# Interleaved scans of a two-layer MetaFormer: other slots for column copies, gate products and output products

## The chip, the cores and the metric

The kernel runs on one core of one Trainium2 chip. The metric is the device time of one execution in microseconds. The kernel before took 1302.23 us, the median of 3 runs (1301.95 to 1303.36).

The core has five engines that run side by side and meet at semaphores: TensorE (PE in the profile), VectorE (DVE), ScalarE (ACT), GpSimd (POOL) and SyncE (SP), which here issues the DMAs. Each works through its own list of instructions in the order in which the program emits them.

## What is computed

Two layers of a MetaFormer on an image of 64 by 64 positions with 96 channels. Each layer is a state-space mixer ("conv") and a small quantized MLP ("ffn"), each with a norm ahead of it and a residual sum behind it. The change touches the mixer of layer 1 and the end of the stage ahead of it. Cut to what matters:

```python
xz = x @ W_in.T
xp, z = xz[..., :192], xz[..., 192:]
xc = silu(conv3x3(xp) + conv_b)                      # all 192 channels to all
x_hw = xc.reshape(B, 192, L)                         # by rows, L = 4096
x_wh = transpose(xc, (0, 1, 3, 2)).reshape(B, 192, L)   # by columns
xs = [x_hw, x_wh, flip(x_hw), flip(x_wh)]            # four directions
x_dbl = einsum('bdl,cd->bcl', xs, x_proj_w)          # step rank 6, B 16, C 16
delta = softplus(dt_proj_w @ x_dbl[:, :6] + dt_proj_b)
# for each channel d and each of 16 states n, along L:
#   h = exp(delta * A) * h + (delta * u) * B
#   y = sum_n h * C
y = scan(...) + D * xs
yy = (y0 + back(y1) + flip(y2) + back(flip(y3))) * silu(z)
out = x + yy @ W_out.T
```

192 channels times 16 states times 4 directions are 12288 recurrences of 4096 steps.

## The kernel before

**Passes.** A pass handles 32 channels and 4 states, on 128 partitions; 6 groups of channels times 4 passes are 24 passes (i = 0 to 23, group g = i // 4, k = i % 4). In a pass two chains run: the row chain (o = 0) and the column chain (o = 1), each forward and then backward over the 4096 steps. A step of a chain (e = 0 to 7) is one DVE scan over 1024 positions, so a pass has 16 scans and the kernel 384.

**The sequence of scans.** The list `seq` (L1891 to L1896) interleaves the two chains: the column chain leads and the row chain follows two steps behind. Position p in `seq` is a scan. `base[i]` is 16i - 2, and the text calls position `base[i] + s` slot s of pass i; slots 16 and more of a pass are slots 0 and more of the next.

**What goes with a scan.** For every p the program emits `scan(p)` for DVE, then `decay(p + 1)` for ACT (the exponential that the next scan needs, L1947), then what the dictionary `plan` holds for p (L2187). A step with e = 4 needs no decay of its own; these are the scans in slots 8 and 13. There are two buffers for decays (`two`), so a decay waits until the scan before the last has ended. As engines take their instructions in order, an instruction put at slot s stands on its own engine in front of everything that is put later.

**The operations that `put` places:**
- `permute(i, a)` (L1936, ACT): copies a quarter of B*du from row order into column order, into `xw`, for the column chain of pass i. It needs all of `xs` of that pass and must wait until `add_columns` of the pass before has read that quarter of `xw`.
- `times_b` (L1930, POOL): B times du, for the next pass but one quarter at a time.
- `add_columns` (L1964, POOL): adds both directions of the column chain, back in row order, into `hs`. It is put at the scan of step NS + a of the column chain.
- `add_rows`, `add_hs`, `add_all` (L1970, L1974, PE): sum both directions of the row chain and `hs` by products with the identity, into two PSUM buffers; `fetch` (L1983, ACT) copies them out; `times_c` (L1987, POOL) multiplies by C; `sum_states` (L1998, PE) adds the states into the accumulator of the group.
- Once in a group: `skip`, `fetch_y`, `store` (L2051, L2057, L2065).
- The gate of a group, in four parts (b, e), two in pass k = 1 and two in pass k = 2: `load_z` (L2025, SP), `product_z` (L2030, PE), `tanh_z` (L2039 to L2041, three operations on ACT), `silu_z` (L2045, POOL). `load_z` writes into the buffer that also holds the group's y until it is stored.
- The early output products of passes 17 to 23: `load_y` (L2075, SP), `early_out` (L2082, L2084, PE), `early_fetch` (L2088, ACT).
- Loads: `load_c` (L1926), `load_part` (B, L1853), `load_du`, `load_dt` (L1909), all issued by SP.

**The stage ahead of the scans.** Layer 0's end, layer 1's convolution and projections are emitted by a planner, `Order`. Every operation has an engine, a cost, what it reads and writes, and for a DMA its size. `run` emits, one at a time, the operation that can start first, and of those that can start at the same time the one of highest rank: the cost of the longest chain of operations that follows, plus a hand-written lead (`LEAD`). The scans stand in this plan as a chain of dummy operations on an engine "SCAN" (`first_pass`, L1213), each with the keys that it needs; so they give rank to what they need.

`project` (L1633) computes, for a unit of 1024 positions, B, C, the step sizes (softplus) and step times u. Channels 0 to 127 are "wide", 128 to 191 "narrow". `by_column` (L1732) also turns the step sizes into column order: the wide ones into `dtc[0]`, the narrow ones into `dtc[1]`. These two lie in the buffers `hs` and `h0` of the scans (L1178). After the last unit:
- `columns(j)` spreads quarter j of the first 32 channels' column steps into `dt1` (L1826);
- `load_b(1, ...)` loads B for pass 1 into `xs(1)` (L1827);
- `store_columns` (L1829) stores the rest of `dtc[0]` and all of `dtc[1]` for later groups.
The row chain's first scan writes `h0`, and so waits until `dtc[1]` has been stored.

Of the kernel before, what the change touches and what calls it, by code (L numbers as in the profile page):

```python
# [39 lines left out]
P = 128  # L40
HW = 64
L = HW * HW
NJ = L // P
CD = 96
DI = 192
# [204 lines left out]
class Net:  # L250
# [962 lines left out]
    def first_pass(self):  # L1213

        o = self.order  # L1220
        pairs = [(c, m) for c in (0, 4) for m in range(2)]
        needs = {0: [("xs0", c) for c in range(NCH)] + [("dt1", k) for k in range(2)] + ["rates"]}
        needs |= {1: [("dt1", 2), ("dt1", 3)]} | {j: [("dt1s", j)] for j in range(2, NS)}
        needs |= {2 * NS: [("DT", p) for p in pairs]}
        needs |= {3 * NS: ["xs1"] + [("DU", p) for p in pairs]}
        needs |= {6 * NS: ["sdtc"] + [(k, p) for k in ("sdt", "sdu", "sdtn", "sdun") for p in pairs]}
        for s in range(6 * NS + 1):
            o.add("SCAN", 2.35, lambda: None, r=needs.get(s, []), w=["scans"])
# [404 lines left out]
    def project(self, c, m, last):  # L1633
# [147 lines left out]
        o.add("SP", 0.65, store_du, r=[du, ("du", n, 0), ("du", n, 1)], w=[("sdu", n)], kb=512)  # L1781
        if m == 1:
            both = [(c, 0), n]
            o.add("SP", 0.65, first_group(lambda: self.dt0, self.dt_d[0]), r=[("sdt", p) for p in both], w=[("DT", p) for p in both], kb=1024)
            o.add("SP", 0.65, first_group(lambda: self.du, self.du_d), r=[("sdu", p) for p in both], w=[("DU", p) for p in both], kb=1024)
# [41 lines left out]
        o.add("SP", 0.65, lambda: self.load_b(1, xs(1), slice(0, L)), r=["xs", *(("B", p) for p in ((0, 0), (0, 1), (4, 0), n))], w=["xs1"], kb=2048)  # L1827

        def store_columns():  # L1829
            keep(dma(self.dt_d[1][GC:P], self.dtc[0][GC:P]))  # L1830
            keep(dma(self.dt_d[1][P:DI], self.dtc[1]))

        narrow = [("dtcn", p, k) for p in ((0, 0), (0, 1), (4, 0), n) for k in range(2)]
        o.add("SP", 1.3, store_columns, r=every + narrow, w=["sdtc"], kb=2560)
# [20 lines left out]
    def scans(self, xs, out):  # L1855
# [14 lines left out]
        with ExitStack() as ctx:  # L1870
# [20 lines left out]
            lead, both, end = 5, 2 * NS, [(1, 4), (1, 5), (0, 2), (1, 6), (1, 7), (0, 3)]  # L1891
            chain = [[(i, o, e) for i in range(n) for e in range(both)] for o in range(2)]
            stop = both * last + 4
            seq = [s for m in range(both * n) for s in (chain[1][m : m + 1] if m < stop else [])
                   + (chain[0][m - 2 : m - 1] if 2 <= m < stop else [])]
            seq += [(last, o, e) for o, e in end] + chain[0][both * last + NS :]  # L1896
# [193 lines left out]
            for f, i0, spots in (  # L2090
                (0, n - 7, ((0, 10, 12), (2, 12, 13))),
                (1, n - 3, ((1, 9, 10), (2, 11, 12), (4, 12, 13))),
            ):
                for m in range(NCH):
                    i, s = divmod(m, len(spots))
                    for do, at_slot in zip((load_y, early_out, early_fetch), spots[s]):
                        early.setdefault((i0 + i, at_slot), []).append((do, (f, m)))
# [13 lines left out]
            for g in range(NG):  # L2111
                for b in range(2):
                    for e in range(2):
                        for f, s in zip((load_z, product_z, tanh_z, silu_z), ((0, 9, 10, 11), (10, 13, 14, 15))[e]):
                            early.setdefault((NK * g + 1 + b, s), []).append((f, (g, b, e)))
# [14 lines left out]
            for i in range(n):  # L2130
# [11 lines left out]
                else:  # L2142
# [8 lines left out]
                    spots(i, sum_states, 19, 22, 23, 26)  # L2151
                    if k == NK - 1:
                        for f, s in ((skip, 26), (fetch_y, 29), (store, 31)):
# [3 lines left out]
                if i:  # L2157
                    for j, s in enumerate((-1, 2, 4, 7)):
                        put(at + s, times_b, i, j)
                    for a, s in enumerate((12, 13, 15, 20)):  # L2160
# [19 lines left out]
            permute(0, 1)  # L2180
# [287 lines left out]
```

## Time and profile before

| | |
|---|---|
| profiled execution | 1301.16 us, span 1299.2 us |
| median of the runs | 1302.23 us |
| stage ahead of the scans | 0 to 329.7 us |
| scans (DVE L1959) | 329.76 to 1222 us |
| tail (output product, MLP of layer 1) | 1222 to 1299.2 us |
| DVE busy | 1142.2 us (88%) |
| PE busy | 1053.5 us (81%) |
| ACT busy | 895.1 us (69%) |
| POOL busy | 844.1 us (65%) |
| mean granted TensorE clock | 0.849 |

A scan takes 2.26 to 2.35 us, and in a full row of them one starts every 2.24 us. Times of the timeline are microseconds from the start of the span. A line of it has start, duration, engine, line of the kernel, operation, what it writes and reads with their shapes, how often, and in brackets the idle time of the engine before it with what ended it. Tile names end in s where the program has several of a kind: `h0s` is `h0`, `hss` is `hs`, `xws` is `xw`; `da` is a decay, `kept` stands for buffers of layer 0 that the scans use again.

### The profile page before, as it was taken

How to read it: one execution, taken by the hardware profiler on the slowest of the kernel's cores; microseconds unless marked ns; L12 is line 12 of the kernel's file. 1: busy time of each engine (PE TensorE's matmuls, PEld its weight loads, DVE VectorE, ACT ScalarE, POOL GpSimd, SP SyncE). 2: the span in 40 equal slices, each digit the busy share in tenths (PEclk: the TensorE clock that was granted, in tenths of full speed). 3: DMA queues.
4: the chain of work that ended last, by engine and by line, in shares of the span. 5: the costliest groups of instructions: out<-in, count | busy, mean ns of one | idle time of the engine just before them, and what ended most of it. 6: DMA issues, size and time to landing. Idle time of an engine off the chain costs nothing. (4 is left out here: it accounts for less than half of the span.)

```text
span 1299.2 us, 11492 instructions
## 1 busy us (share of the span) xinstructions
PE 1053.5 (81%) x3654; PEld 435.4 (34%) x3654; DVE 1142.2 (88%) x899; ACT 895.1 (69%) x1085; POOL 844.1 (65%) x516
## 2 busy tenths in 40 slices
PE   9998988996088777777878877778779887999875
PEld 7632333331033222222223322222224333434443
DVE  6395798668799999999999999999998999999775
ACT  4445656554578877877787877777777877677345
POOL 3000574523578888787888879778887778774445
PEclk9999989985588787888898878878889888888855
DMA  2053010347844483566545473557454474524001
GB/s 72 18 162 98 2 25 13 110 158 237 287 123 131 148 264 123 173 206 204 201 147 175 144 245 100 168 203 232 172 170 157 142 262 129 175 75 130 8 7 43
DMA packets 78912, 183.18 MB, mean 141 GB/s; under 512 B 21503, under 2 KB 34905, under 8 KB 77657
## 3 DMA queue, kind: packets, MB, share of 16 engines
q1 hardware_dynamic: 78152, 182.16, 44.2%
q8 instruction: 31, 0.51, 0.2%
q14 instruction: 41, 0.33, 0.1%
q10 hardware_dynamic: 688, 0.19, 0.1%
HBM read 159.73 MB, written 21.52 MB: 140 GB/s over the span
## 5 line engine op out<-in xcount | busy, mean ns | idle before, releaser
L1987 POOL TENSOR_TENSOR kept<-kept,kept 128x1024 f32<-128x1024 f32 x92 | 216.9, 2357 | 95.0 <-issue 49.4
L1964 POOL TENSOR_TENSOR hss<-h1s,xws 128x1024 f32<-128x1024 f32 x96 | 228.0, 2375 | 77.0 <-DVE xws L1959 74.7
L1970 PE MATMUL hs<-h0s,ident 128*128 128x512 f32 x376 | 229.3, 695 | 48.4 <-DVE h0s L1959 34.7
L1947 ACT ACTIVATE da<-dt1s,a 128x1024 f32<-128x1024 f32 x168 | 187.6, 1117 | 71.3 <-DVE xws L1959 58.6
L1959 DVE TENSOR_TENSOR_SCAN xws<-da,xws 128x1024 f32<-128x1024 f32 x96 | 222.3, 2315 | 9.7 <-ACT da L1947 9.5
L1947 ACT ACTIVATE da<-dt0s,a 128x1024 f32<-128x1024 f32 x168 | 187.9, 1119 | 54.8 <-DVE h0s L1959 31.3
L1974 PE MATMUL hs<-hss,ident 128*128 128x512 f32 x376 | 190.3, 598 | 3.0 <-POOL hss L1964 2.9
L1998 PE MATMUL acc<-kept,fold 128*32 128x512 f32 x384 | 102.3, 715 | 100.4 <-POOL kept L1987 97.0
L1959 DVE TENSOR_TENSOR_SCAN h1s<-da,h1s,xws 128x1024 f32<-128x1024 f32 x72 | 167.7, 2330 | 3.2 <-ACT da L1947 3.0
L1983 ACT COPY kept<-hs 128x512 f32<-128x512 f32 x188 | 109.6, 583 | 64.3 <-PE hs L1974 63.7
L1970 PEld LDWEIGHTS hs<-h0s,ident 128*128 128x128 f32 x376 | 73.5, 215 | 177.8 <-issue 106.1
L1974 PEld LDWEIGHTS hs<-hss,ident 128*128 128x128 f32 x376 | 71.6, 192 | 100.4 <-issue 83.8
L1930 POOL TENSOR_TENSOR x1s<-x1s,dus 128x1024 f32<-128x1024 f32 x32 | 75.6, 2364 | 12.0 <-DMA dus<-du 12.0
L1970 PE MATMUL hs<-x1s,ident 128*128 128x512 f32 x128 | 74.2, 664 | 8.3 <-DVE x1s L1959 8.3
L1970 PE MATMUL hs<-x0s,ident 128*128 128x512 f32 x128 | 72.5, 651 | 9.6 <-DVE x0s L1959 9.6
L1959 DVE TENSOR_TENSOR_SCAN x2s<-da,x2s 128x1024 f32<-128x1024 f32 x32 | 74.2, 2320 | 5.3 <-ACT da L1947 4.9
L1959 DVE TENSOR_TENSOR_SCAN x0s<-da,x0s 128x1024 f32<-128x1024 f32 x32 | 74.2, 2317 | 4.7 <-ACT da L1947 4.7
L1959 DVE TENSOR_TENSOR_SCAN x1s<-da,x1s 128x1024 f32<-128x1024 f32 x32 | 74.2, 2318 | 4.5 <-ACT da L1947 4.5
L1930 POOL TENSOR_TENSOR x2s<-x2s,dus 128x1024 f32<-128x1024 f32 x32 | 75.9, 2371 | 0.0
L1970 PE MATMUL hs<-x2s,ident 128*128 128x512 f32 x120 | 66.9, 642 | 5.0 <-DVE x2s L1959 5.0
L1238 POOL MEMSET pairs<- 96x256 f32 x1 | 0.3, 307 | 103.1 <-ACTq L303 103.1
L1930 POOL TENSOR_TENSOR x0s<-x0s,dus 128x1024 f32<-128x1024 f32 x28 | 66.2, 2365 | 0.0
(346 smaller groups left out, 1976.8 us busy)
## 6 DMA issues: line engine op xcount, KB each, us to landing
kept<-bc SPq DMA_DIRECT2D x92, 512.0 KB
x2s<-bc SPq DMA_DIRECT2D x32, 512.0 KB
x0s<-bc SPq DMA_DIRECT2D x28, 512.0 KB
x1s<-bc SPq DMA_DIRECT2D x28, 512.0 KB
dus<-du SPq DMA_DIRECT2D x20, 512.0 KB
dt1s<-dt SPq DMA_DIRECT2D x20, 512.0 KB
dt0s<-dt SPq DMA_DIRECT2D x20, 512.0 KB
kept<-xn SPq DMA_DIRECT2D x24, 384.0 KB
```

Source lines behind the costliest of these rows:

```text
L1238: nc.gpsimd.memset(self.pairs1[:, :, 0 : HW + 2 : HW + 1, :], 0.0)
L1930: keep(nc.gpsimd.tensor_tensor(x, x, du[:, part[j]], ALU.mult))
L1947: keep(nc.scalar.activation(t, dts[o][:, part[j]], AF.Exp, scale=self.a6[:, g, k : k + 1]))
L1959: keep(nc.vector.tensor_tensor_scan(to, da, x, start, ALU.mult, ALU.add))
L1964: keep(nc.gpsimd.tensor_tensor(cols(hs)[:, w, :], grid(h1)[:, w, :], grid(xw)[:, w, :], ALU.add))
L1970: keep(nc.tensor.matmul(t, self.ident, x[:, chunk(m)], start=x is h0, stop=False))
L1974: keep(nc.tensor.matmul(sums[i, m], self.ident, hs[:, chunk(m)], start=False, stop=True))
L1983: keep(nc.scalar.copy(to, sums.pop((i, j * (SC // CH) + h))))
L1987: keep(nc.gpsimd.tensor_tensor(t, t, times_c_by(i, a), ALU.mult))
L1998: keep(nc.tensor.matmul(to, self.fold4, src, start=k == 0, stop=k == NK - 1))
```

## The change

- *First pass.* Its sequence is written out (`first`): the row chain starts after four column scans instead of three, and two of its scans follow each other. From pass 1 on the sequence and `base` are as before.
- *First column copies.* The second one of pass 0 is made by DVE instead of ACT.
- *Narrow step columns.* `store_columns` becomes two operations: the narrow part, in two halves, which needs the narrow copies alone, and the wide part. The load of B for pass 1 becomes two halves. The second half, and the last unit's load of du, also name the narrow copies among what they read.
- *Dummy scans of the planner.* 23 of 2.25 us instead of 25 of 2.35 us, with other needs at other positions.
- *Slots.* `permute` 12 to 11; `sum_states` 26 to 27; `skip` 26 to 24; `fetch_y` 29 to 28; the gate's two parts from (0, 9, 10, 11) and (10, 13, 14, 15) to (3, 7, 8, 9) and (8, 12, 12, 13); the early output products of passes 17 to 20 from (0, 10, 12), (2, 12, 13) to (5, 9, 10), (7, 10, 11), and of passes 21 to 23 as in the diff.

```diff
@@ first_pass
         needs = {0: [("xs0", c) for c in range(NCH)] + [("dt1", k) for k in range(2)] + ["rates"]}
-        needs |= {1: [("dt1", 2), ("dt1", 3)]} | {j: [("dt1s", j)] for j in range(2, NS)}
-        needs |= {2 * NS: [("DT", p) for p in pairs]}
-        needs |= {3 * NS: ["xs1"] + [("DU", p) for p in pairs]}
-        needs |= {6 * NS: ["sdtc"] + [(k, p) for k in ("sdt", "sdu", "sdtn", "sdun") for p in pairs]}
-        for s in range(6 * NS + 1):
-            o.add("SCAN", 2.35, lambda: None, r=needs.get(s, []), w=["scans"])
+        needs |= {1: [("dt1", 2), ("dt1", 3)], 2: [("dt1s", 2)], 3: [("dt1s", 3)]}
+        needs |= {4: ["sdtcn"] + [("DT", p) for p in pairs[0:2]]}
+        needs |= {8: [("DT", p) for p in pairs[2:4]]}
+        needs |= {5: [("xs1", 0)] + [("DU", p) for p in pairs[0:2]], 7: [("xs1", 1), "sdtc"] + [("DU", p) for p in pairs[2:4]]}
+        needs |= {22: [(k, p) for k in ("sdt", "sdu", "sdtn", "sdun") for p in pairs]}
+        for s in range(23):
+            o.add("SCAN", 2.25, lambda: None, r=needs.get(s, []), w=["scans"])
@@ project
+        narrow = [("dtcn", p, k) for p in ((0, 0), (0, 1), (4, 0), n) for k in range(2)]
         if m == 1:
             both = [(c, 0), n]
...
-            o.add("SP", 0.65, first_group(lambda: self.du, self.du_d), r=[("sdu", p) for p in both], w=[("DU", p) for p in both], kb=1024)
+            o.add("SP", 0.65, first_group(lambda: self.du, self.du_d), r=[*(("sdu", p) for p in both), *(narrow if last else [])], w=[("DU", p) for p in both], kb=1024)
...
-        o.add("SP", 0.65, lambda: self.load_b(1, xs(1), slice(0, L)), r=["xs", *(("B", p) for p in ((0, 0), (0, 1), (4, 0), n))], w=["xs1"], kb=2048)
-
-        def store_columns():
-            keep(dma(self.dt_d[1][GC:P], self.dtc[0][GC:P]))
-            keep(dma(self.dt_d[1][P:DI], self.dtc[1]))
-
-        narrow = [("dtcn", p, k) for p in ((0, 0), (0, 1), (4, 0), n) for k in range(2)]
-        o.add("SP", 1.3, store_columns, r=every + narrow, w=["sdtc"], kb=2560)
+        for h in range(2):
+            half = slice(h * L // 2, (h + 1) * L // 2)
+            o.add("SP", 0.65, lambda half=half: self.load_b(1, xs(1), half), r=["xs", *(("B", p) for p in ((0, 0), (0, 1), (4, 0), n)), *(narrow if h else [])], w=[("xs1", h)], kb=1024)
+
+        def store_columns(g, parts):
+            rows = (slice(GC, P), slice(P, DI))[g]
+
+            def f():
+                for i in range(parts):
+                    s = slice(i * L // parts, (i + 1) * L // parts)
+                    keep(dma(self.dt_d[1][rows, s], self.dtc[g][GC * (1 - g) :, s]))
+
+            return f
+
+        o.add("SP", 1.3, store_columns(1, 2), r=narrow, w=["sdtcn"], kb=1024)
+        o.add("SP", 0.65, store_columns(0, 1), r=every + narrow, w=["sdtc"], kb=1536)
@@ scans
-            lead, both, end = 5, 2 * NS, [(1, 4), (1, 5), (0, 2), (1, 6), (1, 7), (0, 3)]
+            both = 2 * NS
             chain = [[(i, o, e) for i in range(n) for e in range(both)] for o in range(2)]
-            stop = both * last + 4
-            seq = [s for m in range(both * n) for s in (chain[1][m : m + 1] if m < stop else [])
-                   + (chain[0][m - 2 : m - 1] if 2 <= m < stop else [])]
-            seq += [(last, o, e) for o, e in end] + chain[0][both * last + NS :]
+            first = [(1, 0), (1, 1), (1, 2), (1, 3), (0, 0), (1, 4), (0, 1), (1, 5), (0, 2), (0, 3), (1, 6), (0, 4), (1, 7), (0, 5)]
+            end = [(1, 4), (1, 5), (0, 2), (1, 6), (1, 7), (0, 3), *((0, e) for e in range(NS, both))]
+            seq = [(0, o, e) for o, e in first]
+            for m in range(both, both * last + NS):
+                seq += [chain[1][m], chain[0][m - 2]]
+            seq += [(last, o, e) for o, e in end]
...
-                (0, n - 7, ((0, 10, 12), (2, 12, 13))),
-                (1, n - 3, ((1, 9, 10), (2, 11, 12), (4, 12, 13))),
+                (0, n - 7, ((5, 9, 10), (7, 10, 11))),
+                (1, n - 3, ((2, 9, 10), (5, 10, 11), (7, 13, 14))),
...
-                        for f, s in zip((load_z, product_z, tanh_z, silu_z), ((0, 9, 10, 11), (10, 13, 14, 15))[e]):
+                        for f, s in zip((load_z, product_z, tanh_z, silu_z), ((3, 7, 8, 9), (8, 12, 12, 13))[e]):
...
-                    spots(i, sum_states, 19, 22, 23, 26)
+                    spots(i, sum_states, 19, 22, 23, 27)
                     if k == NK - 1:
-                        for f, s in ((skip, 26), (fetch_y, 29), (store, 31)):
+                        for f, s in ((skip, 24), (fetch_y, 28), (store, 31)):
...
-                    for a, s in enumerate((12, 13, 15, 20)):
+                    for a, s in enumerate((11, 13, 15, 20)):
                         put(at + s, permute, i, a)
...
-            permute(0, 1)
+            permute(0, 1, nc.vector.tensor_copy)
```

## The prediction

> **What bounds the kernel now.** I read the page's busy table first, then who waited for whom, then the groups of VectorE (DVE), and last the timelines around the largest waits. The chain that ended last covers only the tail of the program and says nothing about the scans.
>
> ```profile
> DVE  6395798668799999999999999999998999999775
>   ACT da L1947: 28.0, 34
>   DMA dt<-h0s: 5.1, 1
> ```
>
> From slice 10 on DVE is nearly full: it runs 384 scans, started one every 2.24 us (two chains take turns), from 329.76 to 1222 us. The other two lines are the view of the scan line: before a scan DVE sat idle 28.0 us for a decay from ScalarE (ACT) and 5.1 us for one DMA. So the scans' missing starts are the whole prize here. I took the start times of all 384 scans from the trace and summed what each step exceeds 2.24 us by. The sum is 34.8 us. I place it by pass i and slot s (scan number 16i-2+s):
> - the first three steps: 6.5
> - slot 1 of passes 2, 3, 6, 7, 10, 11, 14, 15 (after a pass that computed a gate): 2.8, and slot 2 of pass 15: 1.0
> - slot 15 of passes 4, 8, 12, 16: 2.8
> - passes 17 to 23, where early output products are mixed in: 20.8
> - the last scans, which depend on each other: 1.0
>
> The start:
>
> ```profile
> 329.76 2.29 DVE L1959 TENSOR_TENSOR_SCAN h1s<-da,xws 128x1024 f32<-128x1024 f32 x1 [1.41 <-ACT da L1947]
> 332.68 2.35 DVE L1959 TENSOR_TENSOR_SCAN h1s<-da,h1s,xws 128x1024 f32<-128x1024 f32 x1 [0.63 <-ACT da L1947]
> 335.58 2.35 DVE L1959 TENSOR_TENSOR_SCAN h1s<-da,h1s,xws 128x1024 f32<-128x1024 f32 x1 [0.55 <-ACT da L1947]
> 343.01 2.29 DVE L1959 TENSOR_TENSOR_SCAN h0s<-da,x0s 128x1024 f32<-128x1024 f32 x1 [5.08 <-DMA dt<-h0s]
> 345.21 2.33 DVE L1959 TENSOR_TENSOR_SCAN h1s<-da,h1s,xws 128x1024 f32<-128x1024 f32 x1
> ```
>
> The row chain's first scan writes h0s, which still holds the narrow step columns, and waits until their store has landed. How a slot gets late on ACT:
>
> ```profile
> 436.56 0.37 ACT L2039 COPY kept<-z 128x256 f32<-128x256 f32 x1
> 436.82 0.38 ACT L2040 ACTIVATE kept<-z 128x256 f32<-128x256 f32 x1
> 437.23 0.51 ACT L2041 ACTIVATE kept<-kept,columns 128x256 f32<-128x256 f32 x1
> 437.65 1.10 ACT L1947 ACTIVATE da<-dt1s,a 128x1024 f32<-128x1024 f32 x1
> 438.69 1.98 ACT L1936 COPY xws<-x0s 128x1024 f32<-128x1024 f32 x1
> 440.57 1.11 ACT L1947 ACTIVATE da<-dt0s,a 128x1024 f32<-128x1024 f32 x1
> ```
>
> Start to start, a gate's three operations take 1.2, a decay 1.05, a column copy 1.9. A decay may start when the scan two before its own has ended, so a slot holds one decay and 1.2 of other work; slots 7 and 12 have no decay to make and are free. The gate in slot 14 between copies in 13 and 15 is too much, and the decay at 440.57 ends after its scan was due. Worst, pass 17:
>
> ```profile
> 978.75 0.48 ACT L2088 COPY res<-eo 128x384 f32<-128x384 f32 x1 [5.66 <-PE eo L2084]
> ```
>
> ACT stands at a copy whose TensorE (PE) product is late, and the decay behind it starts at 979.13; the scan waits 4.00 us.
>
> **What the Trainium skill says.** *PSUM — Partial Sum Buffer* (Engine vs sequencer instructions): the queues of ScalarE, VectorE and GpSimdE are strict FIFO, and matmuls run in program order. The trace agrees (the decay behind the 5.66 us wait). *DMA: Bandwidth & Descriptors* (Anatomy of one DMA): about 2.0 us plus bytes at 436 GB/s. From the issue at 328.61, the three queued loads and stores are 3.5 MB, an estimate of 10.4 us by that page; the scan was released at 343.0, after 14.4, so I use the trace's rate. *TensorE: Matmul & The Clock Gate* (What's actually happening): an idle array falls to half clock after about 3.4 us. The trace agrees: 0.43 us a matmul in a run, 1.04 after a 3.96 us wait.
>
> **The change, part by part.**
>
> 1. *Narrow columns stored first, row chain one later, second column copy on DVE.* The copy (1.03) fits in the 1.41 us that DVE idles before scan 0. ACT then makes the second decay at once: scans 0 to 2 start at 329.76, 332.0, 334.3. ACT next does decay 1.05, copy 1.9, decay, copy, decay: the fourth decay ends near 336.9, so scan 3 starts there and scan 4 (the first of the row chain) at 339.2, against 345.21 for scan 4 before: 6.0 gained. It needs the narrow store landed by 339.2. POOL ends the narrow copies at 330.40. The trace's packets show dt0s (1 MB) moving from 331 to 335 and 16 KB stores at 0.38 MB/us, so 1 MB right behind it ends at 337.7, plus about 1 to land: just in time. Against it: the loads of du's second half and of xs1's second half queue behind these stores. GpSimd (POOL) multiplies them (2.34 each) and in its queue the first column sum (2.36) stands between; the copy for pass 1 on ACT, now due about 6 us sooner, needs all three. Before, du landed at 348.36. If both land then, the copy can start at 355.4; ACT can wait until 354.0 without making a decay late: 1.4 lost. At 347 nothing, at 352 about 5. I take 1.0 with a doubled scan (0.15): **gain 5.0**, ends 1 and 6.
>
> 2. *Second gate half from slots 13/14 to 12/12, its load from 10 to 8.* In slot 12 ACT has no decay to make: column copy to 12+0.9, gate to about 13+0.4, decay, copy to 14+1.1, next decay by 14+2.2, on time. The load goes ahead of one du part and one xs part in SP's queue, which removes the 3.96 us for which PE waited on kept<-xn in pass 2. The slot 1 and slot 2 excess goes: **gain 3.7**.
>
> 3. *First gate half from 9/10 to 7/8, its load from 0 to 3.* Here I see a new wait:
>
> ```profile
> 422.09 1.02 PE L1974 MATMUL hs<-hss,ident 128*128 128x512 f32 x2
> 423.05 1.06 PE L1998 MATMUL acc<-kept,fold 128*32 128x512 f32 x8
> 423.93 0.62 PE L2030 MATMUL z<-kept,wz 96*32 96x256 f32 x8
> ```
>
> PE comes to this product without a gap; it is 18.3 us of matmuls behind the first fetch. Nothing stands between slots 7 and 9 in PE's order, so it ends where it ended: 424.55, slot 9+1.0 (9+0.75 when slot 1 is no longer late). But ACT is now to read it in slot 8, ahead of the decay for slot 10. Then gate 1.2, decay 1.05: 1.0+1.2+1.05-2.24 = 1.0 us late. Queued behind it: that decay, the fetch of slot 9, and DVE for both. Twelve passes do it (k = 1 and 2 of six groups); eight of them lie outside the late passes: **loss 8**. Ends: 0 if PE is 1.0 earlier than I think, 16 if it is 1.0 later. The earlier load lets load_c go before the wait for the stored y; POOL's 4 to 5 us waits for kept<-bc in passes 5, 9, 13, 17 go, off the path. The gates' POOL products (0.72) move to 9 and 13, ahead of a column sum; POOL is 82% busy (493 of 602 us) and no scan waits for it.
>
> 4. *Group end: skip 26 to 24, fetch of y 29 to 28, last sum_states 26 to 27.* The fetch (0.9) moves into free slot 12, so slot 15 of passes 4, 8, 12, 16 is on time: **gain 2.8**. The first column copy from 12 to 11 is issued in the same ACT gap, only ahead of that fetch.
>
> 5. *Early products at slots 9, 10 (and 13), ahead of the last sum_states.* PE no longer stands at the sum (POOL) before them. They follow the gate product or the last fetch: 2.7 us each warm. Their loads move from 0 and 2 to 5 and 7, still 9 us ahead of use; the slowest load near there, xn in pass 2 (issued 424.78, its product 434.39), took 9.6, so at worst the first is 0.6 late. In 19 and 20 ACT finds both in time: 0 left of 5.0. In 17, 18, 21, 22 the new wait of part 3 comes first (1.0), the first product is then 0.3 late for its copy, and the second pushes the gate of slot 12 to about 12+2, leaving 0.8 in slots 14/15: 2.1 each, 8.4 together of 20.8: **gain 12.4**, ends 6 and 18.
>
> 6. *Order of the stage before.* The planner ranks operations by what follows; almost everything leads to scan 0 and shifts alike. What rises are the narrow softplus, its POOL copies and DT and DU loads (the store was due at scan 24, now 4). No trace row prices that. PE's conv chain, which ends near 291, sets this stage; I take 0, ends -4 (the last narrow operations stand behind 2.3 and 1.7 us waits now) and +4.
>
> Sum: 5.0+3.7-8.0+2.8+12.4 = 15.9. The profiled execution took 1301.16 (1.96 more than its span), so 1285.3; it lies 1.07 under the median of the runs, so I forecast **1286**.
>
> **Rivals.**
> - *No new wait in slot 8.* PE runs the gate product sooner and ACT finds it ready. For it: fetches could come earlier. Against: PE has no gap to close from slot 1 to 9. The 8 and 4 us return: 1274.
> - *The start is given back.* du and xs1 land at 352 and ACT waits for POOL at the first copy of pass 1: 5 less gain. For it: 1.5 MB of wide columns are stored ahead of them. Against: xs1's first load is half as long. 1291.
> - *Slower.* The new ranks put narrow softplus of the earlier units ahead of conv work on ACT and DVE; conv's PSUM banks are freed later, PE's chain of 72 products stalls, and scan 0 starts late by the same amount. From 15.9 us late it decides; DVE's longest waits there now are 7.4 and 12.4 us, so two such are enough. 19 us late gives 1305. Against it: up to 329.7 us ACT is busy 54% and DVE 71% (177.4 and 234.0 of 329.7 us).
>
> **How the numbers follow.** The forecast (own range 1280 to 1290) gets 0.50, no wait in slot 8 0.19, start given back 0.16, slower 0.10; 0.05 for sums that cancel. A measurement here tells about 0.2% (2.6 us) from no change. Faster 0.85, same 0.05, slower 0.10. The range 1273 to 1297 takes in the first rivals and the ends of parts 1, 3 and 5, and leaves out about 2 in 10.
>
> **What would show it.** In the new trace: scan 4 near 339 with no wait for dt<-h0s (part 1); no scan late in slots 1 and 15 of passes up to 16 (2, 4); scans late by 1 us in slot 10 of passes 1, 2, 5, 6, with ACT's L2039 copy waiting for PE z (3); no 4 us wait in pass 17 (5); scan 0 at 330 +-4 (6). A first scan past 345, or gate waits of 2.5 us, would make the prediction wrong.

## The result and the profile after

The changed kernel took 1298.63 us (median of 20 runs, 1287.6 to 1302.33), the kernel before 1302.45 us (20 runs on the same chips, 1296.88 to 1304.54). The ratio is 0.9967 with a 95% interval of 0.9951 to 0.9983: 0.33% faster. The forecast was 1286, its range 1273 to 1297. The profiled execution of the changed kernel took 1298.4 us, its span 1296.6.

The page's busy strip of DVE and, from the view of the scan line, what DVE sat idle for before a scan (us in all, times):

```profile
DVE  7394788558799999999999999999999999999775
...
  ACT da L1959: 19.9, 23
```

The waits for a decay fell from 28.0 us (34 times) to 19.9 (23 times), and the wait for a DMA is gone. The first scans (timeline: start, duration, engine, line):

```profile
339.42 2.27 DVE L1971 TENSOR_TENSOR_SCAN h1s<-da,xws 128x1024 f32<-128x1024 f32 x1
341.80 7.29 DVE L1971 TENSOR_TENSOR_SCAN h1s<-da,h1s,xws 128x1024 f32<-128x1024 f32 x3
349.00 2.26 DVE L1971 TENSOR_TENSOR_SCAN h0s<-da,x0s 128x1024 f32<-128x1024 f32 x1
```

They run without a wait that the view shows, and the row chain's first scan follows 9.58 us after scan 0 (13.25 before, where it was one place earlier). But scan 0 itself starts at 339.42 instead of 329.76. The scans then take 879.7 us instead of 892.5. So 12.8 us were gained in the scans and 9.7 lost ahead of them. Two waits in the scans are new. The gate's first half on ACT:

```profile
576.50 0.37 ACT L2051 COPY kept<-z 128x256 f32<-128x256 f32 x1 [1.85 <-PE z L2042]
576.77 0.39 ACT L2052 ACTIVATE kept<-z 128x256 f32<-128x256 f32 x1
577.19 0.51 ACT L2053 ACTIVATE kept<-kept,columns 128x256 f32<-128x256 f32 x1
577.60 1.10 ACT L1959 ACTIVATE da<-dt1s,a 128x1024 f32<-128x1024 f32 x1
578.64 0.58 ACT L1995 COPY kept<-hs 128x512 f32<-128x512 f32 x1
579.12 1.11 ACT L1959 ACTIVATE da<-dt0s,a 128x1024 f32<-128x1024 f32 x1
```

ACT stands 1.85 us at the product z with a decay queued behind it; that decay, for the scan of slot 10, ends 0.9 us late. The other one is in pass 0: POOL waits for the second half of the loads, ACT waits for POOL, and scan 12 waits for the decay behind the copy:

```profile
359.56 2.35 POOL L1942 TENSOR_TENSOR x1s<-x1s,dus 128x1024 f32<-128x1024 f32 x1 [13.16 <-DMA du<-ye]
...
366.55 1.95 ACT L1948 COPY xws<-x1s 128x1024 f32<-128x1024 f32 x1 [5.22 <-POOL x1s L1942]
368.40 1.11 ACT L1959 ACTIVATE da<-dt1s,a 128x1024 f32<-128x1024 f32 x1
...
369.55 2.35 DVE L1971 TENSOR_TENSOR_SCAN xws<-da,xws 128x1024 f32<-128x1024 f32 x1 [2.50 <-ACT da L1959]
372.46 2.35 DVE L1971 TENSOR_TENSOR_SCAN x0s<-da,x0s 128x1024 f32<-128x1024 f32 x1 [0.56 <-ACT da L1959]
```

### The profile page after: what moved, and what is told of

It is laid out like the page before. It is cut to its first block, busy times and chain, and to the rows that moved or that the text cites. A ratio compares the mean times of both kernels' runs of the same rounds, so it can differ in the third digit from the quotient of the medians.

```text
span 1296.6 us, 11475 instructions
## 1 busy us (share of the span) xinstructions
PE 1058.3 (82%) x3654; PEld 437.4 (34%) x3654; DVE 1143.7 (88%) x900; ACT 892.4 (69%) x1084; POOL 845.3 (65%) x516
## 5 line engine op out<-in xcount | busy, mean ns | idle before, releaser
L1999 POOL TENSOR_TENSOR kept<-kept,kept 128x1024 f32<-128x1024 f32 x92 | 217.0, 2359 | 90.2 <-issue 52.2
L1959 ACT ACTIVATE da<-dt0s,a 128x1024 f32<-128x1024 f32 x168 | 187.6, 1117 | 50.4 <-DVE h0s L1971 19.9
L1986 PE MATMUL hs<-hss,ident 128*128 128x512 f32 x376 | 191.4, 601 | 8.5 <-POOL hss L1976 8.5
L2010 PE MATMUL acc<-kept,fold 128*32 128x512 f32 x384 | 95.4, 704 | 84.5 <-POOL kept L1999 81.4
L1986 PEld LDWEIGHTS hs<-hss,ident 128*128 128x128 f32 x376 | 71.8, 194 | 110.5 <-issue 81.9
L1982 PE MATMUL hs<-x0s,ident 128*128 128x512 f32 x128 | 75.3, 673 | 13.0 <-DVE x0s L1971 13.0
L1948 ACT COPY xws<-x1s 128x1024 f32<-128x1024 f32 x32 | 63.1, 1972 | 5.2 <-POOL x1s L1942 5.2
```

The costliest lines, as they stand in the source:

```text
L1948: keep(copy(grid(xw)[:, w, :], cols(xs[i % 3])[:, w, :]))
L1959: keep(nc.scalar.activation(t, dts[o][:, part[j]], AF.Exp, scale=self.a6[:, g, k : k + 1]))
L1982: keep(nc.tensor.matmul(t, self.ident, x[:, chunk(m)], start=x is h0, stop=False))
L1986: keep(nc.tensor.matmul(sums[i, m], self.ident, hs[:, chunk(m)], start=False, stop=True))
L1999: keep(nc.gpsimd.tensor_tensor(t, t, times_c_by(i, a), ALU.mult))
L2010: keep(nc.tensor.matmul(to, self.fold4, src, start=k == 0, stop=k == NK - 1))
```

## The experiments

In what follows the "last conv product" is the last `ye<-kept,ye` on POOL, near the end of the conv stage; all engines' orders agree between the two kernels up to some us after it. "Late" is the sum over the scans of what a step exceeds 2.24 us by. Each group of kernels ran on one chip with the kernel before beside it, so ratios are to that; its median was 1301.69 (first group), 1300.29 (second), 1302.6 (third).

### Both kernels again

No edit. Three more profiles of each kernel, and ten more times of the changed one.

> The kernel before, unchanged, profiled once more. If the stage ahead of the scans varies by itself with the clock that TensorE is granted, the first scan starts somewhere else than at 329.76 us, by some us either way, with the same instructions in the same order; if the stage is steady, within 0.5 us of it. The scans from first start to last end should repeat 892.4 us within 1.

> The changed kernel, unchanged, once more. Theory one (clock): the first scan, at 339.42 us in the first profile, starts earlier or later by several us, since 5.4 of the 9.7 us were lost where the order of instructions is still that of before. Theory two (the planner's new order): it starts at 339 to 340 again. Both: scans from first start to last end 879.7 us within 1, and 11 to 12 us of late scans in slot 10.

> The kernel before once more, for a further profile. Between two profiles with the same clock in the front, the change took 7.5 us (front +4.0, scans -11.8, end +0.4), while the medians fell by 3.8 and 5.1 us. Theory A (chance of the clock): the time of the last conv product on GpSimd lies anywhere in 279 to 288 us for either kernel; from it to the first scan 49 to 50.3 us here, scans 889 to 892.5 us. Theory B (a kernel's own front): here always under 282 us, in the changed kernel always over 285 us.

> The changed kernel once more, for a further profile. Theory A: the last conv product on GpSimd anywhere in 279 to 288 us, from it to the first scan 51.5 to 53.1 us, scans within 1 us of 880. Theory B: the last conv product always over 285 us.

> The kernel before a third time, with the same expectations: theory A, last conv product anywhere in 279 to 288 us; theory B, under 282 us.

> The changed kernel a third time, with the same expectations: theory A, last conv product anywhere in 279 to 288 us; theory B, over 285 us.

Measured: after_again 1296.55 us (10 runs), ratio 0.9954 (0.9937 to 0.997). The single runs took 1305.43, 1300.67 and 1299.21 (before) and 1297.69 and 1297.38 (after). From the profiles, in us:

| | before, 4 profiles | after, 4 profiles | mean differs by |
|---|---|---|---|
| start to last conv product | 279.51, 285.59, 283.92, 282.64 | 286.34, 285.56, 285.43, 284.33 | +2.5 |
| from there to scan 0 | 50.25, 49.08, 47.75, 49.05 | 53.08, 53.11, 53.12, 53.13 | +4.1 |
| scan 0 to scan 46 (passes 0 to 2) | 109.38, 109.41, 109.46, 109.49 | 108.10, 110.58, 110.08, 111.37 | +0.6 |
| scan 46 to scan 270 (passes 3 to 16) | 505.91, 505.00, 505.08, 504.58 | 506.73, 504.55, 505.91, 505.33 | +0.5 |
| scan 270 to the last scan's end | 277.18, 277.40, 275.98, 274.60 | 264.90, 264.86, 263.98, 264.82 | -11.7 |
| tail | 76.99, 77.02, 76.56, 76.88 | 77.40, 77.38, 77.36, 76.60 | +0.3 |
| span | 1299.23, 1303.49, 1298.74, 1297.25 | 1296.56, 1296.04, 1295.89, 1295.58 | -3.7 |

The first row differs by 6.1 us within one kernel. Here are two profiles of the same kernel before (view of busy time in stretches: PE, PEld, DVE, ACT and POOL busy with instructions in brackets, granted clock, DMA share, GB/s); the first is that of the prediction, the second its repeat:

```profile
240.00:265.00 25.00, 25.00 (x77) 8.86 (x75) 20.51 (x29) 20.04 (x33) 11.13 (x7) 1.00 0.35 111
```

```profile
240.00:265.00 25.00, 23.01 (x52) 8.09 (x48) 16.99 (x23) 14.60 (x24) 9.86 (x7) 0.86 0.30 90
```

In the same 25 us TensorE finished 77 matmuls at a clock of 1.00, or 52 at 0.86. The loss comes in pieces: in the second profile the clock is 0.50 from 243.0 to 246.4 us and 0.51 from 256.6 to 260.0 (1.00 in both in the first), matmuls there take 1.06 us that take 0.59 in the first, and PE waits 1.99 us for DVE once, where it did not wait:

```profile
255.97 1.41 PE L1653 MATMUL bank<-kept,kept 128*102 128x512 f32 x2 [1.99 <-DVE kept L1620]
```

Ahead of this (L1699, at 240.42 and 239.39) the second profile was 1.0 us behind the first, and after it (L1695, at 261.27 and 254.81) 6.5 us.

Over all 18 profiles of this study the last conv product lay between 279.38 and 287.67 us, the lowest from a variant with the changed kernel's front (gate_old below). So its place is no property of one of the two kernels: theory A. The mean of 2.5 us between four profiles each is not told apart from chance: over all 18, the seven with the new list of dummy scans average 284.7 us and the eleven others 283.7. That the change has no part in it isn't shown either. Without this row the profiles would give a gain of 6.2 us, and the medians fell by 3.8 and 5.1. The second row is another matter: 53.1 in every one of the four profiles of the changed kernel, 47.8 to 50.3 before.

### The planner's list alone, and all but the list

```diff
 list_only (on the kernel before): the hunk of first_pass alone
-        needs |= {2 * NS: [("DT", p) for p in pairs]}
+        needs |= {4: ["sdtcn"] + [("DT", p) for p in pairs[0:2]]}
...
-        for s in range(6 * NS + 1):
-            o.add("SCAN", 2.35, lambda: None, r=needs.get(s, []), w=["scans"])
+        for s in range(23):
+            o.add("SCAN", 2.25, lambda: None, r=needs.get(s, []), w=["scans"])
 no_list (on the changed kernel): the same hunk undone
```

> The kernel before with one part of the change alone: the planner's list of dummy scans (23 of 2.25 us, with the new needs, in place of 97 of 2.35 us). Sequence, loads, stores and slots are those of before. Theory A (the list reorders the stage before): VectorE's first scan comes about 4.0 us later after the last product of the conv stage on GpSimd (ye<-kept; 49.1 us in the repeat of before, 53.1 us in the repeat of after), two column copies hss<-xws of GpSimd stand ahead of the two products xws<-dt1s,xws, and the median is 3 to 5 us over the one of before. Theory B (the later first scan comes from the moved stores and the new first sequence): first scan within 0.5 us of before by the same measure, median within 1.5 us of before.

> The changed kernel with the planner's old list of 97 dummy scans; all else (halved load, stores, first sequence, slots) as changed. Theory A: 49 us instead of 53 from the last conv product on GpSimd to the first scan; the scans themselves as in the changed kernel (about 880 us from the first start to the last end), so the median is about 4 us below the repeat of after: 1292 to 1293 against 1296.6. Theory B: first scan still about 53 us after that product, median about 1296.6.

(The list of before has 25 dummy scans, not the 97 of these texts.) Measured: list_only 1305.6 us, ratio 1.0042 (1.0025 to 1.0059), so slower than before; from the last conv product to scan 0 it needs 52.24 us, and its first row scan is late by 5.6 us (5.1 to 5.2 before). no_list 1291.49 us, ratio 0.9934 (0.9912 to 0.9956); 49.41 us to scan 0, and scans of 880.3 us. The list alone moves scan 0 by 3.2 us (mean of before: 49.0), and undoing it takes 3.7 off the changed kernel's 53.1; without it, all the other edits leave scan 0 where it was. By medians alone no_list and the changed kernel are not apart (0.9934 and 0.9954, intervals overlap); the trace separates them. Theory A.

Two limits. The size is not the same in every execution: gate_old below, with the same front as the changed kernel, needed 51.53 us in its one profile. And the list names some keys that only other parts of the change write (the halves of the load, the narrow store), as the old one names the whole load; in list_only and no_list such a key holds nothing back and gives no rank. Still, in list_only PE, DVE, ACT and POOL each leave the order of before at the same instruction as in the changed kernel.

How the order does it shows on POOL (timelines of list_only, then of the repeat of before):

```profile
299.07 3.44 POOL L1737 COPY hss<-xws 128x512 f32<-128x512 f32 x2 [12.53 <-DVE xws L1724]
302.49 3.12 POOL L1728 TENSOR_TENSOR xws<-dt1s,xws 128x512 f32<-128x512 f32 x2
```

```profile
299.41 3.85 POOL L1727 TENSOR_TENSOR xws<-dt1s,xws 128x512 f32<-128x512 f32 x2 [12.56 <-DVE xws L1723]
303.22 2.73 POOL L1736 COPY hss<-xws 128x512 f32<-128x512 f32 x2
```

The new list makes the step columns urgent, so the planner puts their copies ahead of the products of step and u. The PE instructions that spread these products wait 3 us longer and move behind four projection matmuls. In the repeat of after the last run of spreading matmuls then starts at 323.62 instead of 321.69 (repeat of before): 1.9 of the 4.0 us between these two profiles. Another 1.7 us are lost in the narrow softplus, where ACT's order has changed in the same way. A square of that softplus (one of the ACT steps that it is made of; L1719, in the changed kernel L1720) stood ahead of a copy of the step columns and now stands behind it (ACT, repeat of before, then of after):

```profile
326.53 0.72 ACT L1719 ACTIVATE h1s<-h1s,columns 128x512 f32<-128x512 f32 x1 [1.65 <-DVE ye L1718]
328.93 0.59 ACT L1806 COPY dt1s<-bank 128x512 f32<-128x512 f32 x1 [1.68 <-DMA dt1s<-hss]
```

```profile
330.88 0.59 ACT L1808 COPY dt1s<-bank 128x512 f32<-128x512 f32 x1 [4.05 <-issue]
331.37 0.72 ACT L1720 ACTIVATE h1s<-h1s,columns 128x512 f32<-128x512 f32 x1
```

So DVE waits longer for the softplus's last square. Repeat of before, then of after:

```profile
330.17 0.69 DVE L1721 SCALAR_TENSOR_TENSOR ye<-h1s,ye 128x512 f32<-128x512 f32 x1 [2.30 <-ACT h1s L1720]
...
332.23 1.03 DVE L1936 COPY xws<-x0s 128x1024 f32<-128x1024 f32 x1
334.67 2.29 DVE L1959 TENSOR_TENSOR_SCAN h1s<-da,xws 128x1024 f32<-128x1024 f32 x1 [1.41 <-ACT da L1947]
```

```profile
333.84 0.69 DVE L1722 SCALAR_TENSOR_TENSOR ye<-h1s,ye 128x512 f32<-128x512 f32 x1 [4.02 <-ACT h1s L1721]
...
335.90 2.85 DVE L1948 COPY xws<-x0s 128x1024 f32<-128x1024 f32 x2
338.67 2.27 DVE L1971 TENSOR_TENSOR_SCAN h1s<-da,xws 128x1024 f32<-128x1024 f32 x1
```

Scan 0 used to wait 1.41 us for ACT. It now waits for DVE's own list: two copies behind the narrow softplus, which stood 4.02 us at a square of ACT. So the idle time in which the second copy was to hide is gone, and the copy, which took 1.91 us, adds the last 0.3 us. The new list is what made the loss: no_list has the same two copies and needs 49.41 us.

### The slots alone, the new first sequence, and the stores

```diff
 slots (on the kernel before): the hunks of early output, gate, sum_states, skip, fetch_y and permute
+                (0, n - 7, ((5, 9, 10), (7, 10, 11))),
+                        for f, s in zip((load_z, product_z, tanh_z, silu_z), ((3, 7, 8, 9), (8, 12, 12, 13))[e]):
+                        for f, s in ((skip, 24), (fetch_y, 28), (store, 31)):
...
 seq_slots (on slots): the new sequence and DVE's second copy
+            first = [(1, 0), (1, 1), (1, 2), (1, 3), (0, 0), (1, 4), (0, 1), (1, 5), (0, 2), (0, 3), (1, 6), (0, 4), (1, 7), (0, 5)]
+            permute(0, 1, nc.vector.tensor_copy)
 stores_first (on seq_slots): the narrow store apart and first; no halved load, no new need of du's load
+        o.add("SP", 1.3, store_columns(1, 2), r=narrow, w=["sdtcn"], kb=1024)
+        o.add("SP", 0.65, store_columns(0, 1), r=every + narrow, w=["sdtc"], kb=1536)
```

> Before, with the new slots alone (permute, gate, early products, skip, fetch of y, last sum); the stage ahead, the first pass and its first copies as before. If the slots bring what the first profiles show, the scans take 892.4 - 10 = 882 to 883 us and the first pass keeps its 6.5 us of late starts. If the planner's new order is what ate the gain, the whole is faster than the changed kernel: about 1292; if the stage ahead only varies by itself, it is within 3 us of the changed kernel, near 1297.

> Before with the new first sequence, the second column copy on VectorE and all slots of the change, but neither the planner's list nor the changed stores and loads of the stage before. Theory A: first scan as in before (49 us after the last conv product). If the narrow stores that go first are what the new first sequence lives on, its first row scan waits as before for the columns' store, so the first pass shows a stall of about 5 us, and the time is that of the slots alone, about 1294.5; if their place in the queue does not matter, no stall over 1 us at the first row scan and about 1292.5.

> The kernel of seq_slots with the narrow columns' store split off and put ahead of the wide one, without the halved load and the new need of the first products' load. Theory A (the narrow store first is what the row chain waits for; the stall of scans 12 and 13 comes from the halved, delayed load): first row scan late by less than 0.5 us instead of 3.5, scans 12 and 13 not late, scans about 876 us instead of 879.9, median about 3.5 us below that of seq_slots, 1288 to 1289. Theory B (the queue only changes what waits: what the row chain gains, the loads behind the stores lose): scans 12 and 13 late by 2 to 3 us as in the changed kernel, scans within 1 us of 880, median within 1.5 us of 1292.3.

| | median us (runs) | ratio (interval) | conv product to scan 0 | first row scan late | scans 12, 13 late | scans |
|---|---|---|---|---|---|---|
| slots | 1294.55 (6) | 0.9942 (0.9923 to 0.9962) | 49.07 | 5.1 | 0 | 880.6 |
| seq_slots | 1292.25 (6) | 0.9938 (0.9917 to 0.9959) | 48.04 | 3.5 | 0 | 879.9 |
| stores_first | 1290.32 (6) | 0.9919 (0.9891 to 0.9946) | 49.39 | 0.85 | 0 | 876.9 |
| changed kernel (after_again) | 1296.55 (10) | 0.9954 (0.9937 to 0.997) | 53.11 | 0 | 3.1 | 880.0 |

The slots alone bring the scans from 890.9 (mean of four) to 880.6; everything in the first pass and ahead of it takes only another 0.3 off in the changed kernel (mean of four 880.3). The median of slots, 2.0 us below the changed kernel's, doesn't tell its two expectations apart. The new sequence without the new stores (seq_slots) still waits at its first row scan, though 3.5 us and not the 5 that were expected:

```profile
345.56 2.29 DVE L1961 TENSOR_TENSOR_SCAN h0s<-da,x0s 128x1024 f32<-128x1024 f32 x1 [3.36 <-DMA dt<-h0s]
```

Putting the narrow store first (stores_first) takes 2.6 of these 3.5 us away without any late scan at 12 or 13, and the scans shorten by 3.0. So the 3.1 us at scans 12 and 13 of the changed kernel do not come from the store's place. What stores_first leaves out are the planner's list, the halved load of B for pass 1, and the narrow copies as a need of that half and of du's last load. no_list, which differs from stores_first in these loads alone, parts them: its scans 12 and 13 are late by 2.0 us and its first row scan by 0.03. So the loads cost 2.0 us at scans 12 and 13 and take the last 0.8 off the first row scan; the other 1.1 of the 3.1 come with the list. That is theory A for the larger part. The intervals of the four medians overlap; this reading rests on the traces, one for each variant.

### Where the gate inputs stand

```diff
 gate9 (on the changed kernel)
-                        for f, s in zip((load_z, product_z, tanh_z, silu_z), ((3, 7, 8, 9), (8, 12, 12, 13))[e]):
+                        for f, s in zip((load_z, product_z, tanh_z, silu_z), ((3, 7, 9, 10), (8, 12, 12, 13))[e]):
 slots_gate (on slots):      ((3, 7, 9, 10), (8, 12, 13, 14))
 gate_old (on the changed kernel): ((0, 9, 10, 11), (10, 13, 14, 15))
 seq_gate (on seq_slots):    ((1, 5, 8, 9), (7, 10, 12, 13))
```

> The changed kernel with the first gate half's tanh at slot 9 and its POOL product at slot 10 instead of 8 and 9. If ACT waits there for the product of TensorE, which comes at slot 9 + 1.0, the twelve late scans of slot 10 go: scans 868 to 869 us in place of 879.7, and about 11 us less in all. If the lateness of slot 10 has another cause, or is only moved to the next slot, the scans stay at 878 us or more.

> The slots of the change on the front and first sequence of before, with the gate inputs' first half in slots 3, 7, 9, 10 (tanh one slot after the wait that slot 8 made) and the tanh and silu of the second half one slot later too (8, 12, 13, 14). Theory A (ScalarE has room, only the place of the two waits was wrong): no late scan in slot 10 and none in slots 14 and 15 of the passes 2, 6, 10, 14; late scans sum to about 12 us instead of 20.4, median about 1286 to 1288. Theory B (ScalarE and TensorE have no room in these passes, a wait taken away in one slot comes back in another): slots 14, 15 or 1 of those passes show 1.3 to 1.7 us, late scans sum to 18 to 20 us, median 1293 to 1295.

> The changed kernel with the gate inputs' slots of before (0, 9, 10, 11 and 10, 13, 14, 15); all else as changed. Prediction's own account (the first half's new place costs 12 x 1.0 us, the second half's gains 3.7 us): no late scan in slot 10, slots 1 of two passes in four late by 0.35 us again, the scans about 8 us shorter than the changed kernel's 880 us, so about 872, and the median about 1288 to 1290 against 1296.6 of the changed kernel. Rival (ScalarE's work of these passes has nowhere to go, a wait taken out of slot 10 returns in slots 14, 15 and 1): scans within 3 us of 880, median 1294 to 1297.

> The kernel of seq_slots with both halves of the gate inputs earlier: load, product, tanh, silu in slots 1, 5, 8, 9 and 7, 10, 12, 13. Theory A (the waits of slots 10, 14 and 15 come from ScalarE standing behind a product that TensorE had not reached, or that its load had not reached; ScalarE has room in slots 8 and 12): no scan over 0.3 us late in slots 10, 14, 15 of the passes 1 to 15; the scans take about 868 to 870 us instead of 879.9, median about 1281. Theory B (ScalarE is full over slots 11 to 15: three column copies of 1.95 us and five decays of 1.05 us are 11.1 of 11.2 us, and 1.2 us of tanh do not fit): slot 15 is late by 0.8 us in passes 1, 2, 5, 6 and so on, as in the kernel with slots 8, 12, 13, 14; scans about 875 us, median about 1287.

| | median us (runs) | ratio (interval) | scans | what is late in passes k = 1 and 2 up to 16 |
|---|---|---|---|---|
| changed kernel | 1296.55 (10) | 0.9954 (0.9937 to 0.997) | 880.0 | slot 10 by 0.9 to 1.6 |
| gate9 | 1291.51 (6) | 0.9922 (0.9904 to 0.9941) | 880.1 | slots 14 and 15 of k = 2, together by 1.3 to 1.7 |
| slots_gate | 1287.5 (6) | 0.9896 (0.9878 to 0.9914) | 876.3 | slot 15 of both by 0.82 |
| gate_old | 1287.88 (6) | 0.9905 (0.9879 to 0.9931) | 874.8 | slot 1 after both by 0.3 to 0.4 |
| seq_gate | 1279.95 (6) | 0.9836 (0.9808 to 0.9864) | 869.3 | nothing over 0.12 |

gate9 takes the wait out of slot 10; in passes k = 1 it is gone, in k = 2 it returns four slots later, behind the second half's product. PE waits 1.5 to 2.4 us there for the product's load; in the changed kernel, whose scans slot 10 had already held up, it waits at most 0.6 us for it. ACT of gate9:

```profile
585.35 0.37 ACT L2051 COPY kept<-z 128x256 f32<-128x256 f32 x1 [2.44 <-PE z L2042]
...
586.46 1.10 ACT L1959 ACTIVATE da<-dt1s,a 128x1024 f32<-128x1024 f32 x1
...
589.35 1.10 ACT L1959 ACTIVATE da<-dt0s,a 128x1024 f32<-128x1024 f32 x1
```

Its median is lower than the changed kernel's (the intervals overlap) although its profile shows no shorter scans; the profiled run was the longest of its six, and what the others gained isn't shown. In slots_gate the product is in time, and the three operations stand between the copies of slots 13 and 15 (ACT, no idle time at all):

```profile
548.89 1.93 ACT L1936 COPY xws<-x0s 128x1024 f32<-128x1024 f32 x1
550.74 0.36 ACT L2039 COPY kept<-z 128x256 f32<-128x256 f32 x1
551.00 0.38 ACT L2040 ACTIVATE kept<-z 128x256 f32<-128x256 f32 x1
551.41 0.51 ACT L2041 ACTIVATE kept<-kept,columns 128x256 f32<-128x256 f32 x1
551.83 1.10 ACT L1947 ACTIVATE da<-dt0s,a 128x1024 f32<-128x1024 f32 x1
552.87 1.10 ACT L1947 ACTIVATE da<-dt1s,a 128x1024 f32<-128x1024 f32 x1
```

That is theory B's place with half its price: the time fell into theory A's range, the mechanism was B's. Undoing the whole move (gate_old) shortens the changed kernel's scans by 5.5 us against the mean of its four profiles (880.3). That is more than the rival's 3 and less than the 8.3 of the prediction's account. In the passes up to 16 the gain is 5.2 us, where steps 2 and 3 give 4.3; in passes 17 to 23 it is 0.3, where 4 was expected, because other waits stand there (2.4 us in slot 12 of pass 21). In seq_gate both products and loads come earlier, so that ACT finds them done in slots 8 and 12, where it is idle:

```profile
566.02 0.36 ACT L2041 COPY kept<-z 128x256 f32<-128x256 f32 x1
...
574.57 0.36 ACT L2041 COPY kept<-z 128x256 f32<-128x256 f32 x1
...
576.11 1.12 ACT L1949 ACTIVATE da<-dt1s,a 128x1024 f32<-128x1024 f32 x1 [0.37 <-DVE xws L1961]
```

No wait for PE here, and after the second trio ACT itself has 0.37 us to spare. (In passes 5 and 13 ACT waits 0.2 and 0.5 us for the second product, and no scan is late by it.) The scans take 10.6 us less than in seq_slots. So ScalarE has room for the gate in these passes, but only where its input is ready: theory A.

### All parts together

```diff
 all_parts (on the changed kernel): the hunk of first_pass undone, and
-                        for f, s in zip((load_z, product_z, tanh_z, silu_z), ((3, 7, 8, 9), (8, 12, 12, 13))[e]):
+                        for f, s in zip((load_z, product_z, tanh_z, silu_z), ((1, 5, 8, 9), (7, 10, 12, 13))[e]):
-                    for a, s in enumerate((11, 13, 15, 20)):
+                    for a, s in enumerate((11, 13, 15, 20) if i > 1 else (13, 15, 17, 20)):
```

> The changed kernel with the planner's old list of dummy scans, both halves of the gate inputs earlier (1, 5, 8, 9 and 7, 10, 12, 13) and the first pass's column copies in slots 13, 15, 17, 20 instead of 11, 13, 15, 20. If the list, slot 10 and the copy that waits in the first pass are independent costs (4 + 11 + 2 us in the traces), the first scan stands 49 us after the last conv product, scans 12 and 13 are on time, the scans take about 867 us, and the median is 1278 to 1281. If they are one debt of ScalarE, the scans take 875 to 880 us and the median is 1287 to 1292.

Measured: 1277.69 us (5 runs, 1273.23 to 1278.28), ratio 0.9817 (0.9791 to 0.9844). Scan 0 stands 49.40 us after the last conv product, scans 12 and 13 are on time, the scans take 864.8 us. From the view of the scan line:

```profile
  ACT da L1958: 6.2, 8
```

6.2 us of waits for a decay are left of the changed kernel's 19.9. Against the means of the changed kernel's profiles that is 3.7 us ahead of scan 0 and 15.5 in the scans. So the three costs are not one debt of ScalarE: the gains nearly add (3.7, the 10.6 of seq_gate and 3.1 at scans 12 and 13). The moved column copies were not run alone. With the list undone and the copies where the change put them (no_list), 2.0 us are left at scans 12 and 13; here none is.

## Why the forecast was wrong

The steps of the prediction sum to 15.9 us. Sorted by stretches of the program, and set beside the four profiles of each kernel:

| stretch | forecast | measured | forecast too good by |
|---|---|---|---|
| up to the last conv product (step 6) | 0 | +2.5 | 2.5 |
| from there to scan 0 (step 6) | 0 | +4.1 | 4.1 |
| passes 0 to 2 (step 1, a part of 2 and 3: -5.0 - 0.35 + 2.0) | -3.35 | +0.6 | 3.9 |
| passes 3 to 16 (steps 2, 3, 4: -3.35 + 6.0 - 2.8) | -0.15 | +0.5 | 0.6 |
| passes 17 to 23 (step 5) | -12.4 | -11.7 | 0.7 |
| tail | 0 | +0.3 | 0.3 |
| sum | -15.9 | -3.7 | 12.2 |

**Step 6 failed.** It said "No trace row prices that" and took 0 with ends of 4 us either way. In its place the runs show a loss of 4.1 us between the last conv product and scan 0 (which then stood at 337.5 to 339.4 us), and the new list of dummy scans makes most of it: put in alone it costs 3.2 us (52.2 us to scan 0), and undone it gives back 3.7 (49.4). Step 6 expected the narrow softplus to rise in the order and everything else to shift alike; on ACT a square of that softplus went behind a copy of the step columns. The rival "slower" looked for a loss, but in the conv stage, where the orders are the same; it is behind that, where the last products of step and u and the narrow softplus lie on the way to scan 0. The further 2.5 us in the conv stage look like chance of the clock as far as 18 profiles tell; whether the change has a part in them stays open. The profile from which the forecast was made had the shortest conv stage of its kernel's four.

**Step 1 came out in its main sum, partly by luck, and was mis-sized in its last term.** The row chain's scan came 9.6 us after scan 0, no wait for the store was left, and scan 0 to scan 4 shrank from 15.4 to 9.6 us: 5.9 gained where 6.0 was worked out. But the way there was another. Step 1 let the first scans follow each other after 2.24 us and then had scan 3 wait for its decay. In the profile that decay ended at 345.75, 1.0 us before scan 3 started at 346.74, and the scans, each of which needs the one before, started 2.38, 2.46 and 2.48 us apart. Two errors cancelled. The second column copy did not fit into the 1.41 us of idle DVE either: it took 1.91 us, not 1.03, and the idle time was gone.

The mis-sized term is the wait of the first column copy. Taken as 1.0 us plus a doubled scan of 0.15, it measured 2.5 + 0.7 us at scans 12 and 13. The prediction gave "at 347 nothing, at 352 about 5" for the landing of the loads. Counted from scan 0, POOL's product was released 9.66 us less than its 359.56, at 349.9 on the prediction's clock, against the 348.36 it took. With 349.9 its own working gives a copy at 356.9 and 2.9 us lost: the steps were right and the landing was 1.5 us late. Here the rival "start is given back" was right in kind. no_list beside stores_first shows that the halved load and its new need made 2.0 us of it, not the stores. (The prediction's 10.4 us for three transfers took a fit that its page gives for DMAs issued by GpSimd, and SyncE issues these; its sum uses the trace's rate and does not rest on that figure.)

In the three repeats passes 0 to 2 took 2.0 to 3.3 us longer than in the first profile (108.1). Most of it lies in pass 1, whose slots 5, 6 and 10 are late by 0.3, 0.8 and 1.6 us there and by 0, 0 and 0.6 in the first profile. It goes with the clock: from 372.7 to 379.5 us it is 0.50 in the repeat and 0.96 in the first profile, four sums (PE L1986) take 3.78 us instead of 1.98, and ACT's fetch behind them waits. No step priced that.

**Step 3 held.** The wait came in slot 10 of the passes k = 1 and 2, with ACT at the copy of z, by 0.9 us in most of them (11.7 us in twelve passes of the first profile; 1.0 each was forecast). The rival that saw no wait there is refuted. gate9 and slots_gate show what step 3 did not say: a wait that is taken out of slot 10 can return in slot 14 or 15, because its load and the copies of slots 11, 13 and 15 leave no other room there.

**Steps 2, 4 and 5 held.** In the first profile slots 1 and 15 of the passes 1 to 16 are on time but for slot 15 of passes 6 and 10 (0.7 each; in the repeats it is slot 15 of passes 2, 10 or 14, by 0.4 to 0.7); the 4 us wait of pass 17 is gone; 9.2 us are left of the late passes where 8.4 were forecast (after_again).

## What to carry to other kernels

A planner that is given new needs or another list of what follows can reorder a stage that the diff doesn't touch, and scan 0 then pays for urgency that was granted to something else: compare the emitted order of each engine around the hand-over before costing such an edit at nothing. When an operation is moved to an earlier place, its producer and its load must come early enough too, or the engine stands at it and the wait goes on to the next instruction in its list (1.85 us for the product here, 0.9 us for the scan). A forecast of 1% made from one profile needs a second one: a stage that depends on the granted clock can differ by 6 us between executions of the same program.

## What the runs showed of the hardware

- Executions whose engines have the same order up to there reached the last conv product at 279.4 to 287.7 us in 18 profiles. For one pair of the kernel before the loss is worked out: in two stretches of 3.4 us the clock was 0.50 and 0.51 instead of 1.00, matmuls of one shape took 1.06 us instead of 0.59, and with a wait of 1.99 us the execution fell back by 5.4 us.
- A column copy of DVE or a copy of POOL (L1737) that began while the other engine's copy ran took 0.7 to 0.9 us longer. In the repeat of after DVE's first copy, begun first, took 1.02 us; POOL's, begun 0.15 us later, 1.80; DVE's second, of the same size as its first and begun beside that one, 1.91; POOL's next 1.78. The repeat of before has no second DVE copy, and there POOL's next one took 1.07. What the two engines share there isn't shown.
- Scans that depend on the scan just before them start 2.38 to 2.48 us apart, with 0.11 to 0.13 us of idle DVE between them, against 2.24 us for two chains that take turns.
